# Taking TensorE's turns and bank waits one iteration later in a graph layer's edge loop

## The chip, the cores and the metric

The kernel runs on one core of a Trainium2 chip. The metric is the device time of one execution in microseconds, lower is better. The profile's names for the engines are used throughout: PE is TensorE, PEld its weight loads, DVE is VectorE, ACT is ScalarE, POOL is GpSimd, SP is SyncE. A *post* is the semaphore update by which an instruction tells the other engines that it is done.

## The reference

One layer of message passing over 12,500 nodes and 400,000 edges that are sorted by their destination, all in float32, residual added at the end:

```
h  = max(layernorm(x), 0)
y0 = h0 @ W_l1_0 * a ; y1 = h1 @ W_l1_1 * a          (nodes: 64 scalars, 32 vectors of 3)
w  = silu(edge16 @ fc_W1) @ fc_W2                    (edges: 192 weights each)
ys = y[edge_src]
mid = [w_a*ys0*e0, w_d*(ys1 . e1), (w_b*ys0) x e1, w_c*e0 x ys1]     (384 numbers an edge)
z  = zeros.at[edge_dst].add(mid)
out = x + C_S*(h @ W_sc * a) + C_X*(z @ W_l2 * a)
```

## The kernel before

A first stage goes over the nodes, writes the rows y to `y_d` in DRAM and keeps x plus the self term in `acc` in SBUF. Meanwhile POOL gathers rows of x for 22 batches whose y rows are made later on the chip instead of gathered (`gather_x`, L345).

Then comes the edge loop. The edges lie in 3,125 tiles of 128. Four tiles (`GT`) are a batch, so there are 782 batches, and iteration b of the loop issues work of several batches at once. The order on PE, ACT and DVE is written out by hand (`manual_schedule`): each engine runs its instructions in just the order in which the loop issues them. POOL runs ahead on its own.

- POOL: `load(b + 8)` issues four indirect DMAs, one a tile, that gather rows of y into a buffer `yg` (nine buffers). A buffer is free for the next gather when ACT has lifted it and DVE's `tmp` and `both` have read it. A made batch gathers nothing.
- PE: `weigh(b + 2)` makes the weights of a batch in one of two pairs of banks, `pw` (L566). It must wait until DVE has done the products of batch b, which read the same `pw`. `sums(b)` multiplies the products with a 0/1 selector and adds them in a bank `pz` (L603); a group of tiles shares one `pz` bank, 24 tiles (6 batches) in the first 1,824 tiles, called the wide part here, 12 tiles (3 batches) in the narrow part behind it. Two `pz` banks are used in turn.
- ACT: `pw` (L567) copies the edge's vector behind the weights as soon as `weigh` has posted; then it runs the evictions of `leaving`, that is what PE wrote in the iteration before (`all_leave`), then `yge` (L484), the lifting of the gathered rows. DVE can't begin a batch before ACT's `pw`.
- DVE: `dot` (L489, L491), `multiply` (L495 to L501), and every third batch `select` (L583), which makes the selector of 12 tiles by comparing the numbers 0 to 127 with the edges' relative destinations. The numbers lie in columns 384 to 511 of the `pz` banks.

At a group's end e, ACT evicts the sums in iteration e + 1 (`zs`, L609). PE turns them in the same iteration e + 1 (`turn`, L617), ACT evicts the turned sums at e + 2 (`za`, L621) and PE multiplies them with the output weights at e + 2 too (`map_sums`, L630). Turns, maps, the edge network's first layer (`hidden`, L550, in every second iteration) and the made batches' own turns and maps (L689, L700 to L702) all take the next of two shared banks `px`; so one iteration can use both, and a bank is used again as soon as ACT has evicted it.

The made batches are those with b a multiple of 32, up to 704.

Of the kernel before, what the change touches and what calls it, by code (L numbers as in the profile page):

```python
# [10 lines left out]
F32 = mybir.dt.float32  # L11
I32 = mybir.dt.int32
AF = mybir.ActivationFunctionType
ALU = mybir.AluOpType
# [4 lines left out]
P = 128  # L19
M0 = 64  # L20
M1 = 32
# [4 lines left out]
ZC = 384  # L26
GT = 4
BT = 32
WN = 128
TG = 12  # L30
EG = 8
WIDE = 3, 5
GN = 8
HN = 2
RB = 22
RS = 32
LO = D - P
EPS = 1e-5
C_S = math.sin(math.pi / 8.0)
# [4 lines left out]
def kernel(  # L44
# [19 lines left out]
    nc = tc.nc  # L64
# [36 lines left out]
    nr = max(0, min(RB, (NB - 1) // RS - 1))  # L101
    RT = nr * GT
    xr_d = dram.tile([max(nr, 1) * P, GT * D + 1], F32, name="xr_d")

    def made(b):

        return b // RS - 1 if b % RS == 0 and 0 < b <= nr * RS else None

    z_d = dram.tile([ZR, ZC], F32, name="z_d")

# [197 lines left out]
    with (  # L308
# [20 lines left out]

        def find_x():  # L330

            of = src_sb[:, RS * GT:RS * GT * (nr + 1)].rearrange("p (r c) -> p r c", c=RS * GT)[:, :, 0:GT]
            whole = nrp.tile([P, nr, GT], I32, name="whole")
            nc.vector.tensor_scalar(whole, of, 7, None, ALU.arith_shift_right)
            nc.vector.tensor_copy(hi_f.rearrange("p (r c) -> p r c", c=GT), whole)
            nc.vector.tensor_copy(lo_f.rearrange("p (r c) -> p r c", c=GT), of)
            nc.vector.scalar_tensor_tensor(lo_f, hi_f, -float(P), lo_f, op0=ALU.mult, op1=ALU.add)

        def gather_x(lo, hi):

            for r in range(lo, hi):
                xr = nrx.tile([P, GT * D + 1], F32, name="xr")
                for k in range(GT):
                    c = (r + 1) * RS * GT + k
                    nc.gpsimd.indirect_dma_start(  # L345
                        out=xr[:, k * D:(k + 1) * D], out_offset=None, in_=x,
                        in_offset=bass.IndirectOffsetOnAxis(ap=src_sb[:, c:c + 1], axis=0))
                xrs[r] = xr
# [134 lines left out]
        for k in range(n):  # L483
            nc.scalar.activation(yge[:, k, :], yg[:, k, :], AF.Copy, scale=e4v[:, k, 0:1])  # L484
# [8 lines left out]
    def multiply(pr, both, tmp, wt, yg, yge, n):  # L493

        nc.vector.tensor_mul(both[:, :n, :], wt[:, :n, 96:160], yg[:, :n, 0:M0])  # L495
# [5 lines left out]
        nc.vector.tensor_mul(pr[:, :n, 96:192].rearrange("p t (c u) -> p t c u", c=3),  # L501
                             wt[:, :n, M0:96].unsqueeze(2).to_broadcast([P, n, 3, M1]),
                             yge[:, :n, M0:].rearrange("p t (c u) -> p t c u", c=3))

    with (
# [15 lines left out]
        def next_px():  # L521
            turns["px"] += 1
            return pxs[turns["px"] % 2]
# [4 lines left out]
        def tiles_of(b):  # L528
            return list(range(b * GT, min((b + 1) * GT, T)))
# [46 lines left out]
            o = g % EG * TG + k * GT  # L576
            return raws[g // EG][:, o:o + GT, :]

        def select(u, pz):

            n = min(TG, T - u * TG)
            sels[u] = selp.tile([P, TG, WN], F32, name="sel")
            nc.vector.tensor_tensor(sels[u][:, 0:n, :], pz[:, ZC:].unsqueeze(1).to_broadcast([P, n, WN]),  # L583
                                    drel[:, u * TG:u * TG + n].unsqueeze(2).to_broadcast([P, n, WN]), ALU.is_equal)

        def dots_of(b):
            dots[b] = part.tile([P, GT, 4, M1], F32, name="tmp")
            dot(dots[b], wts[b], rows[b], len(tiles_of(b)))

        def products(b):  # L590
            pr = prod.tile([P, GT, ZC], F32, name="pr")
            both = part.tile([P, GT, M0], F32, name="both")
            multiply(pr, both, dots.pop(b), wts.pop(b), rows.pop(b), lifted.pop(b), len(tiles_of(b)))
            prs[b] = pr

        def sums(b):
# [15 lines left out]
        def turn(g):  # L612

            zs = z_sb.pop(g)
            pt = next_px()[:, 0:3 * P].rearrange("p (k c) -> p k c", k=3)
            for k in range(3):
                nc.tensor.transpose(pt[:, k, :], zs[:, P * k:P * (k + 1)], ident)  # L617

            def out_of():
                za = post.tile([P, 3, P], F32, name="za")  # L620
                nc.scalar.activation(za, pt, AF.Copy)  # L621
                zT[g] = za
            leaving.append(out_of)
# [97 lines left out]

        def plan(r):

            end = (r + 1) * RS - 9
            last = end - (end + 1) % 6
            first = last - 6 * (GT - 1)
            for when, b, f in ([(at_start, first - 6, made_load), (on_vector, first - 3, made_moments),
                                (on_vector, first - 1, made_reciprocal)]):
                when.setdefault(max(b, 0), []).append(lambda f=f: f(r))
            for k in range(GT):  # L730
                j = first + 6 * k
                for when, b, f in ((on_vector, j - 1, made_rows), (on_tensor, j, made_turn), (on_tensor, j + 2, made_map),
                                   (on_vector, j + 4, made_attr), (on_scalar, j + 5, made_leave)):
                    when.setdefault(b, []).append(lambda f=f, k=k: f(r, k))

        for r in range(nr):
# [13 lines left out]
        with order:  # L750
# [6 lines left out]
                all_leave()  # L757
            if NQ == 1:
                any_far(next_px()[0:1, 0:1])
            for b in range(min(2, NB)):  # L760
                weigh(b)
                lift_rows(b)
            for pz in pzs:
                nc.vector.tensor_copy(pz[:, ZC:], iota[:, 0:WN])
            dots_of(0)
            products(0)
            select(0, pzs[0])
# [47 lines left out]
    with (  # L815
# [11 lines left out]
        with tc.For_i(0, n, 1) as _:  # L827
# [4 lines left out]
            with tc.For_i(0, TP // GT, 1) as g:  # L832
# [31 lines left out]
                dot(tmp, pw, yg, GT)  # L864
                pr = fp.tile([P, GT, ZC], F32, name="f_pr")
                both = fp.tile([P, GT, M0], F32, name="f_both")
                multiply(pr, both, tmp, pw, yg, yge, GT)
# [81 lines left out]
```

## Time and profile before

| what | us |
|---|---|
| median of 3 runs | 5222.7 |
| lowest and highest run | 5202.25, 5230.44 |
| the profiled execution's own time | 5204.84 |
| its span, first to last instruction | 5203.0 |
| PE, DVE, POOL, ACT busy | 4180.4, 3441.9, 2959.6, 1764.7 |
| granted clock of TensorE, mean | 0.857 |

The span is that of one profiled execution. In rows of groups the columns are: line, engine, operation, out<-in by the program's names, shapes, xcount, then busy us and mean ns of one, then the engine's idle time just before them and what ended most of it. In rows of the timeline: start us, duration us, engine, line, operation, names, shapes, xcount, and in brackets the idle time before and what ended it. "issue" and "remote" mean that the profile shows nothing on this core's engines that ended the wait. The profile records a float32 matmul as two rows.

### The profile page before, as it was taken

Reading aid. Unit: us, or ns where it says so; the run is one execution under the profiler, and the core shown is the slowest. Engines: PE = TensorE matmul, PEld = TensorE weight load, DVE = VectorE, ACT = ScalarE, POOL = GpSimd, SP = SyncE. Lnnn points to the kernel's source line nnn. Section 1 sums busy time; section 2 is a strip of 40 time slices with the busy share of each in tenths; the row PEclk is TensorE's granted clock in tenths of the full one; section 3 lists DMA queues with packets and bytes.
Section 4 is the critical chain, followed back from the end, with each engine's and each line's share of the span. In section 5 each row is a group of like instructions: output and inputs, shape, how many; then the busy total and the mean of one; then the engine's idle time right before and its main releaser. Section 6 shows DMA issues by size and latency. Waiting matters only on the chain. (4 is left out here: it accounts for less than half of the span.)

```text
span 5203.0 us, 55078 instructions
## 1 busy us (share of the span) xinstructions
PE 4180.4 (80%) x16329; PEld 2384.2 (46%) x16329; DVE 3441.9 (66%) x7529; ACT 1764.7 (34%) x5580; POOL 2959.6 (57%) x3137
## 2 busy tenths in 40 slices
PE   4478888787888888888888878888888888888888
PEld 3334444444444444444444444444444444544444
DVE  4456667666666666776666666676767666766667
ACT  3323333333333333332333333333333333333333
POOL 4455655555555555555555555555555555655553
PEclk7778888888888888888888888888888888888888
DMA  5322222222222222222222222222222222232222
GB/s 180 115 57 58 61 58 62 58 60 60 57 60 59 60 61 57 59 61 60 57 60 58 60 57 57 60 60 58 60 54 61 58 59 57 61 94 57 57 57 58
DMA packets 227720, 333.84 MB, mean 64 GB/s; under 512 B 54714, under 2 KB 171526, under 8 KB 227158
## 3 DMA queue, kind: packets, MB, share of 16 engines
q0 software_dynamic: 150000, 256.20, 19.9%
q1 hardware_dynamic: 63618, 65.63, 4.0%
q10 hardware_dynamic: 13796, 8.44, 0.5%
q8 instruction: 130, 2.13, 0.2%
q14 instruction: 176, 1.44, 0.1%
HBM read 306.83 MB, written 23.22 MB: 63 GB/s over the span
## 5 line engine op out<-in xcount | busy, mean ns | idle before, releaser
L540 POOL DMA_INDIRECT yg<-y_d,src_sb x3037 | 2871.3, 945 | 2115.7 <-ACT yge L484 784.9
L603 PE MATMUL pz<-pr,sel 128*128 128x384 f32 x6250 | 2510.0, 548 | 58.4 <-issue 54.7
L603 PEld LDWEIGHTS pz<-pr,sel 128*128 128x128 f32 x6250 | 1259.2, 212 | 1032.0 <-issue 491.5
L489 DVE TENSOR_TENSOR tmp<-yg,pw 128x384 f32<-128x384 f32 x760 | 418.6, 551 | 1523.1 <-ACT pw L567 1292.7
L567 ACT ACTIVATE pw<-raw 128x12 f32<-128x12 f32 x782 | 141.9, 182 | 3289.3 <-issue 2801.2
L484 ACT ACTIVATE yge<-yg,raw 128x160 f32<-128x160 f32 x3037 | 1044.0, 421 | 0.0
L566 PE MATMUL pw<-w,hT 64*128 64x192 f32 x6250 | 839.5, 392 | 73.7 <-issue 24.1
L566 PEld LDWEIGHTS pw<-w,hT 64*128 64x128 f32 x6250 | 572.6, 212 | 545.1 <-issue 313.4
L497 DVE TENSOR_TENSOR pr<-both,pw 128x768 f32<-128x768 f32 x782 | 737.9, 944 | 0.0
L550 PE MATMUL px<-xe,w 32*128 32x512 f32 x782 | 522.9, 756 | 189.4 <-ACT os L635 137.1
L491 DVE TENSOR_REDUCE tmp<-tmp 128x128 f32<-128x384 f32 x782 | 464.1, 594 | 26.9
L583 DVE TENSOR_TENSOR sel<-pz,drel 128x1536 f32<-128x1536 f32 (+1 forms) x261 | 455.2, 1744 | 0.0
L501 DVE TENSOR_TENSOR pr<-pw,yge 128x384 f32<-128x384 f32 x782 | 428.0, 547 | 0.0
L617 PE MATMUL px<-ident,zs 128*128 128x128 f32 x555 | 112.7, 319 | 358.9 <-ACT zs L609 341.3
L500 DVE TENSOR_TENSOR pr<-pw,yge 128x256 f32<-128x256 f32 x782 | 326.6, 418 | 13.0 <-ACT yge L484 12.3
L495 DVE TENSOR_TENSOR both<-pw,yg 128x256 f32<-128x256 f32 x760 | 314.8, 414 | 0.0
L550 PEld LDWEIGHTS px<-xe,w 32*128 32x128 f32 x782 | 130.7, 209 | 345.5 <-ACT os L635 163.4
L630 PE MATMUL px<-wc,za 128*128 128x96 f32 x1110 | 165.5, 289 | 145.3 <-ACT za L621 137.7
L617 PEld LDWEIGHTS px<-ident,zs 128*128 128x128 f32 x555 | 74.2, 159 | 446.9 <-ACT zs L609 395.9
L630 PEld LDWEIGHTS px<-wc,za 128*128 128x128 f32 x1110 | 161.5, 205 | 207.4 <-ACT za L621 155.1
L555 ACT ACTIVATE hT<-px 128x512 f32<-128x512 f32 x391 | 229.3, 587 | 1.9 <-PE px L550 1.7
L496 DVE TENSOR_TENSOR pr<-pw,tmp 128x128 f32<-128x128 f32 x782 | 219.4, 281 | 0.0
(118 smaller groups left out, 1739.2 us busy)
## 6 DMA issues: line engine op xcount, KB each, us to landing
yg<-y_d,src_sb POOLq DMA_INDIRECT x3037
xe<-in_e SPq DMA_DIRECT2D x196, 128.0 KB
y_d<-ys ACTq DMA_DIRECT2D x12, 640.0 KB
xr_d<-xr SPq DMA_DIRECT2D x22, 320.5 KB
acc<-in_x SPq DMA_DIRECT2D x11, 640.0 KB
xm<-xr_d SPq DMA_DIRECT2D x22, 320.0 KB
out<-acc SPq DMA_DIRECT2D x11, 640.0 KB
raw<-in_e SPq DMA_DIRECT2D x32, 192.0 KB
```

The source lines that it names most:

```text
L484: nc.scalar.activation(yge[:, k, :], yg[:, k, :], AF.Copy, scale=e4v[:, k, 0:1])
L489: nc.vector.tensor_tensor(tmp[:, :n, 0:3, :], y1, wt[:, :n, NW:NW + 3].unsqueeze(3).to_broadcast([P, n, 3, M1]), ALU.mult)
L491: nc.vector.tensor_reduce(tmp[:, :n, 3, :], tmp[:, :n, 0:3, :].rearrange("p t c u -> p t u c"), AX.X, ALU.add)
L497: nc.vector.tensor_mul(pr[:, :n, 192:ZC].rearrange("p t (c u) -> p t c u", c=3), both[:, :n, :].unsqueeze(2).to_broadcast([P, n, 3, M0]), ...
L500: nc.vector.tensor_mul(pr[:, :n, 0:M0], wt[:, :n, 0:M0], yge[:, :n, 0:M0])
L501: nc.vector.tensor_mul(pr[:, :n, 96:192].rearrange("p t (c u) -> p t c u", c=3), wt[:, :n, M0:96].unsqueeze(2).to_broadcast([P, n, 3, M1]) ...
L540: nc.gpsimd.indirect_dma_start(out=yg[:, k, :], out_offset=None, in_=y_d, in_offset=bass.IndirectOffsetOnAxis(ap=src_sb[:, t:t + 1], axis=0))
L550: nc.tensor.matmul(ph, w1[r, :], xe[r, :], start=True, stop=True)
L566: nc.tensor.matmul(pw[:, k, 0:NW], hT[r, o:o + P], w2[r, :], start=True, stop=True)
L583: nc.vector.tensor_tensor(sels[u][:, 0:n, :], pz[:, ZC:].unsqueeze(1).to_broadcast([P, n, WN]), drel[:, u * TG:u * TG + n].unsqueeze(2).to ...
L603: nc.tensor.matmul(z_ps[g], sels[t // TG][:, t % TG, :], pr[:, k, :], start=first, stop=last)
L630: nc.tensor.matmul(px[:, lo:hi], za[:, k, :], wc[:, k, lo:hi], start=k == 0, stop=k == 1)
```

## The change

Sums' turns move. `turn(g)` comes at e + 2 in place of e + 1 and writes into the group's own `pz` bank, whose sums ACT has evicted an iteration before. `map_sums` follows at the next odd iteration at least two later, and the add to `acc` two after that; at the end of the program all three keep the old distance. The shared banks `px` are now used once an iteration: `hidden` in even iterations, maps and the made batches' turns and maps in odd ones. For this the made batches are spread anew: 16 of them 24 batches apart in the wide part (before 14, 32 apart), 6 of them 48 apart in the narrow part, where the four tiles of one are handled 12 iterations apart in place of 6, with 6 between turn and map in place of 2.

The numbers 0 to 127 for the selector leave `pz`: 32 of them lie behind the weights of each of the four tiles in both `pw` (column 224 on). `select` reads them there, in the bank of the batch that DVE is at, and comes between `dots_of` and `products` in place of behind `products`. `both` moves from `multiply` to `dot`, ahead of the reduction.

```diff
+SP = 256 - WN // 4
-RB = 22
-RS = 32
+RB = 16, 6
+RS = 24, 48
...
-    def dot(tmp, wt, yg, n):
+    def dot(tmp, both, wt, yg, n):
 
         y1 = yg[:, :n, M0:].rearrange("p t (c u) -> p t c u", c=3)
         nc.vector.tensor_tensor(tmp[:, :n, 0:3, :], y1, wt[:, :n, NW:NW + 3].unsqueeze(3).to_broadcast([P, n, 3, M1]),
                                 ALU.mult)
+        nc.vector.tensor_mul(both[:, :n, :], wt[:, :n, 96:160], yg[:, :n, 0:M0])
         nc.vector.tensor_reduce(tmp[:, :n, 3, :], tmp[:, :n, 0:3, :].rearrange("p t c u -> p t u c"), AX.X, ALU.add)
...
-            nc.vector.tensor_tensor(sels[u][:, 0:n, :], pz[:, ZC:].unsqueeze(1).to_broadcast([P, n, WN]),
-                                    drel[:, u * TG:u * TG + n].unsqueeze(2).to_broadcast([P, n, WN]), ALU.is_equal)
+            for_each = pw[:, :, SP:].unsqueeze(1).to_broadcast([P, n, GT, WN // GT])
+            nc.vector.tensor_tensor(sels[u][:, 0:n, :].rearrange("p t (k c) -> p t k c", k=GT), for_each,
+                                    drel[:, u * TG:u * TG + n].unsqueeze(2).unsqueeze(3).to_broadcast(
+                                        [P, n, GT, WN // GT]), ALU.is_equal)
...
-            pt = next_px()[:, 0:3 * P].rearrange("p (k c) -> p k c", k=3)
+            pt = pzs[g % 2][:, 0:3 * P].rearrange("p (k c) -> p k c", k=3)
...
-                turns_at.setdefault(e + 1, []).append(g)
-                maps_at.setdefault(e + 2, []).append(g)
-                adds_at.setdefault(e + (4 if e + 4 < NB else 3), []).append(g)
+                at_end = e + 4 >= NB
+                t = e + (1 if at_end else 2)
+                m = t + (1 if at_end else 2 if (t + 2) % 2 else 3)
+                turns_at.setdefault(t, []).append(g)
+                maps_at.setdefault(m, []).append(g)
+                adds_at.setdefault(m + (1 if at_end else 2), []).append(g)
...
                     dots_of(b + 1)
+                    if k == K - 1:
+                        select(u + 1, wts[b + 1])
                     products(b + 1)
-                    if k == K - 1:
-                        select(u + 1, pzs[(group_at[b * GT] + 1) % 2])
```

On PE, in the wide part, at a group's end. L603 is `sums`, L617 `turn`, L550 `hidden`, L566 `weigh`, L630 `map_sums`, L700 to L702 a made batch's map; the numbers tell the two `pz` and the two `px` apart. Before:

```order
L603 MATMUL pz_1674<-pr,sel 128x384 x4
L617 MATMUL px_1675<-ident,zs 128x128 x3
L550 MATMUL px_1676<-xe,w_98 128x512
L566 MATMUL pw_1672<-w_99,hT 128x192 x4
L603 MATMUL pz_1674<-pr,sel 128x384 x4
L630 MATMUL px_1675<-wc,za 128x96
L630 MATMUL px_1675<-wc,za 128x64
L630 MATMUL px_1675<-wc,za 128x96
L700 MATMUL px_1676<-wn_96,m_t 128x64
```

Changed, with the lines eight to twelve further down (L615 `sums`, L629 `turn`, L558 `hidden`, L574 `weigh`, L642 `map_sums`, L712 the made batch's map):

```order
L615 MATMUL pz_1675<-pr,sel 128x384 x4
L629 MATMUL pz_1676<-ident,zs 128x128 x3
L712 MATMUL px_1678<-wn_96,m_t 128x64
L713 MATMUL px_1678<-wn_97,m_t 128x96
L714 MATMUL px_1678<-a_sb,m_t 128x98
L574 MATMUL pw_1673<-w_99,hT 128x192 x4
L615 MATMUL pz_1675<-pr,sel 128x384 x4
L558 MATMUL px_1677<-xe,w_98 128x512
L574 MATMUL pw_1674<-w_99,hT 128x192 x4
L615 MATMUL pz_1675<-pr,sel 128x384 x4
L642 MATMUL px_1678<-wc,za 128x96
```

The turn now stands in the bank of the group that ended, while `sums` go to the other one; `hidden` has one `px` bank in even iterations, and the maps have the other in odd ones, with two iterations between turn and map.

On DVE, in a batch with a selector. L489 is the product for `tmp`, L491 its reduction, L495 `both`, L496 to L501 the products that PE sums, L583 `select`. Before:

```order
L489 TENSOR_TENSOR tmp<-yg,pw_1671 128x4x96
L491 TENSOR_REDUCE tmp<-tmp 128x4x32
L495 TENSOR_TENSOR both<-pw_1671,yg 128x256
L496 TENSOR_TENSOR pr<-pw_1671,tmp 128x4x32
L497 TENSOR_TENSOR pr<-both,pw_1671 128x4x192
L500 TENSOR_TENSOR pr<-pw_1671,yge 128x4x64
L501 TENSOR_TENSOR pr<-pw_1671,yge 128x4x96
L583 TENSOR_TENSOR sel<-pz_1673,drel 128x1536
```

Changed, with L497, L500 and L499 in place of L489, L491 and L495, L504 to L509 for the products and L592 for `select`:

```order
L497 TENSOR_TENSOR tmp<-yg,pw_1673 128x4x96
L499 TENSOR_TENSOR both<-pw_1673,yg 128x256
L500 TENSOR_REDUCE tmp<-tmp 128x4x32
L592 TENSOR_TENSOR sel<-pw_1673,drel 128x1536
L504 TENSOR_TENSOR pr<-pw_1673,tmp 128x4x32
L505 TENSOR_TENSOR pr<-both,pw_1673 128x4x192
L508 TENSOR_TENSOR pr<-pw_1673,yge 128x4x64
L509 TENSOR_TENSOR pr<-pw_1673,yge 128x4x96
```

The selector stands ahead of the four products, on whose last one PE's next `weigh` for that `pw` waits.

More of the change, by code (lines that the diff above doesn't have):

```diff
@@ L99 @@
     y_d = dram.tile([N, D], F32, name="y_d")
-    nr = max(0, min(RB, (NB - 1) // RS - 1))
+    n1 = max(0, min(RB[0], wide // GT // RS[0] - 2, (NB - 1) // RS[0] - 1))
+    from2 = wide // GT // RS[0] * RS[0] + RS[1]
+    n2 = max(0, min(RB[1], (NB - 1 - from2) // RS[1] + 1))
+    made_at = [RS[0] * (r + 2) for r in range(n1)] + [from2 + RS[1] * r for r in range(n2)]
+    nr = n1 + n2
     RT = nr * GT
@@ L105, in made @@
     def made(b):
-        return b // RS - 1 if b % RS == 0 and 0 < b <= nr * RS else None
+        return made_at.index(b) if b in made_at else None
     z_d = dram.tile([ZR, ZC], F32, name="z_d")
@@ L330, in find_x @@
         def find_x():
-            of = src_sb[:, RS * GT:RS * GT * (nr + 1)].rearrange("p (r c) -> p r c", c=RS * GT)[:, :, 0:GT]
             whole = nrp.tile([P, nr, GT], I32, name="whole")
-            nc.vector.tensor_scalar(whole, of, 7, None, ALU.arith_shift_right)
+            for r, n, step in ((0, n1, RS[0]), (n1, n2, RS[1])):
+                if n:
+                    c = made_at[r] * GT
+                    of = src_sb[:, c:c + ((n - 1) * step + 1) * GT].rearrange("p (m c) -> p m c", c=GT)[:, ::step, :]
+                    nc.vector.tensor_scalar(whole[:, r:r + n, :], of, 7, None, ALU.arith_shift_right)
+                    nc.vector.tensor_copy(lo_f[:, r * GT:(r + n) * GT].rearrange("p (r c) -> p r c", c=GT), of)
             nc.vector.tensor_copy(hi_f.rearrange("p (r c) -> p r c", c=GT), whole)
-            nc.vector.tensor_copy(lo_f.rearrange("p (r c) -> p r c", c=GT), of)
             nc.vector.scalar_tensor_tensor(lo_f, hi_f, -float(P), lo_f, op0=ALU.mult, op1=ALU.add)
@@ L343, in gather_x @@
                 for k in range(GT):
-                    c = (r + 1) * RS * GT + k
+                    c = made_at[r] * GT + k
                     nc.gpsimd.indirect_dma_start(
@@ L490, in dot, with multiply @@
                                 ALU.mult)
+        nc.vector.tensor_mul(both[:, :n, :], wt[:, :n, 96:160], yg[:, :n, 0:M0])
         nc.vector.tensor_reduce(tmp[:, :n, 3, :], tmp[:, :n, 0:3, :].rearrange("p t c u -> p t u c"), AX.X, ALU.add)
-    def multiply(pr, both, tmp, wt, yg, yge, n):
-        nc.vector.tensor_mul(both[:, :n, :], wt[:, :n, 96:160], yg[:, :n, 0:M0])
+    def multiply(pr, both, tmp, wt, yge, n):
         nc.vector.tensor_mul(pr[:, :n, M0:96], wt[:, :n, 160:NW], tmp[:, :n, 3, :])
@@ L722, in plan @@
         def plan(r):
-            end = (r + 1) * RS - 9
+            b = made_at[r]
+            step, lag = (6, 2) if b * GT <= wide else (12, 6)
+            end = b - 7 - lag
             last = end - (end + 1) % 6
-            first = last - 6 * (GT - 1)
+            first = last - step * (GT - 1)
             for when, b, f in ([(at_start, first - 6, made_load), (on_vector, first - 3, made_moments),
@@ L730, in plan @@
             for k in range(GT):
-                j = first + 6 * k
-                for when, b, f in ((on_vector, j - 1, made_rows), (on_tensor, j, made_turn), (on_tensor, j + 2, made_map),
-                                   (on_vector, j + 4, made_attr), (on_scalar, j + 5, made_leave)):
+                j = first + step * k
+                for when, b, f in ((on_vector, j - 1, made_rows), (on_tensor, j, made_turn), (on_tensor, j + lag, made_map),
+                                   (on_vector, j + lag + 2, made_attr), (on_scalar, j + lag + 3, made_leave)):
                     when.setdefault(b, []).append(lambda f=f, k=k: f(r, k))
@@ L759 @@
                 any_far(next_px()[0:1, 0:1])
+            for pw in pws:
+                nc.vector.tensor_copy(pw[:, :, SP:], iota[:, 0:WN].rearrange("p (k c) -> p k c", k=GT))
             for b in range(min(2, NB)):
@@ L762 @@
                 lift_rows(b)
-            for pz in pzs:
-                nc.vector.tensor_copy(pz[:, ZC:], iota[:, 0:WN])
             dots_of(0)
+            select(0, wts[0])
             products(0)
-            select(0, pzs[0])
             last_batch = [(t - 1) // GT for t in ends]
@@ L863 @@
                 tmp = fp.tile([P, GT, 4, M1], F32, name="f_tmp")
-                dot(tmp, pw, yg, GT)
                 pr = fp.tile([P, GT, ZC], F32, name="f_pr")
                 both = fp.tile([P, GT, M0], F32, name="f_both")
-                multiply(pr, both, tmp, pw, yg, yge, GT)
+                dot(tmp, both, pw, yg, GT)
+                multiply(pr, both, tmp, pw, yge, GT)
                 for k in range(GT):
```

12 lines of the change are left out of this document (7 added, 5 removed).

## The prediction

> **What bounds the kernel now.** I read the page first: its first line, then the groups of POOL's gathers and of ACT's `pw`.
>
> ```profile
> PE 4180.4 (80%) x16329; PEld 2384.2 (46%) x16329; DVE 3441.9 (66%) x7529; ACT 1764.7 (34%) x5580; POOL 2959.6 (57%) x3137
> L540 POOL DMA_INDIRECT yg<-y_d,src_sb x3037 | 2871.3, 945 | 2115.7 <-ACT yge L484 784.9 <-issue 782.1 <-ACT pw L567 161.0
> L567 ACT ACTIVATE pw<-raw 128x12 f32<-128x12 f32 x782 | 141.9, 182 | 3289.3 <-issue 2801.2
> ```
>
> PE is the busiest engine and still idle for a fifth of the span. ACT is idle far longer, 3289.3 us of it in front of `pw`, most of it put down to nothing. The list of PE's waits says for what, with total us, times and longest:
>
> ```profile
> PE px L617 <- ACT zs L609: 341.3, 82, 9.7
> PE px L630 <- ACT za L621: 137.7, 27, 9.8
> PE px L550 <- ACT os L635: 137.1, 37, 6.1
> PE px L689 <- ACT os L635: 65.3, 17, 6.6
> ```
>
> These are just the waits that the change is made for: 341.3 + 137.7 + 137.1 + 65.3 = 681 us in 163 waits. The question is whether they are a cause or a symptom. They are 4.2 us in the mean, with single ones near 10. So I looked at ACT, which does the evictions behind `pw`, in the timeline from 2040 to 2080 us, and at POOL and PE beside it, one fence each:
>
> ```profile
> 2050.26 0.18 ACT L567 ACTIVATE pw<-raw 128x12 f32<-128x12 f32 x1 [7.47 <-issue]
> 2050.37 0.47 ACT L609 ACTIVATE zs<-pz 128x384 f32<-128x384 f32 x1
> ...
> 2078.46 0.18 ACT L567 ACTIVATE pw<-raw 128x12 f32<-128x12 f32 x1 [9.75 <-issue]
> ```
>
> ```profile
> 2049.84 0.94 POOL L540 DMA_INDIRECT yg<-y_d,src_sb  x1 [0.30 <-issue]
> 2052.72 0.94 POOL L540 DMA_INDIRECT yg<-y_d,src_sb  x1 [1.94 <-issue]
> ...
> 2075.16 0.95 POOL L540 DMA_INDIRECT yg<-y_d,src_sb  x1 [0.30 <-issue]
> ```
>
> ```profile
> 2043.43 0.92 PE L566 MATMUL pw<-w,hT 64*128 64x192 f32 x8
> 2044.28 2.85 PE L603 MATMUL pz<-pr,sel 128*128 128x384 f32 x8
> 2050.90 0.90 PE L617 MATMUL px<-ident,zs 128*128 128x128 f32 x3 [3.77 <-ACT zs L609]
> 2051.73 2.07 PE L550 MATMUL px<-xe,w 32*128 32x512 f32 x2
> 2053.73 1.65 PE L566 MATMUL pw<-w,hT 64*128 64x192 f32 x8
> 2055.32 5.16 PE L603 MATMUL pz<-pr,sel 128*128 128x384 f32 x8
> ...
> 2069.35 0.92 PE L566 MATMUL pw<-w,hT 64*128 64x192 f32 x8
> ...
> 2072.98 1.12 PE L550 MATMUL px<-xe,w 32*128 32x512 f32 x2
> 2074.03 0.92 PE L566 MATMUL pw<-w,hT 64*128 64x192 f32 x8
> ```
>
> ACT's `pw` at 2050.26 needs the `weigh` that PE shows as ended at 2043.43 + 0.92 = 2044.35. It starts 5.9 us later, when POOL has come to the end of a run of gathers. PE's wait for `zs`, an eviction of 0.47 us, is the tail of that wait. At 2078.46 it is the same, 8.2 us behind the `weigh` of 2069.35, and there PE waited for no eviction: it went on to `hidden` and the next `weigh`, and ACT still stood until POOL's run had ended at 2075.16 + 0.95. So a `weigh`'s post reaches ACT late while POOL issues gathers, whether PE waits or not.
>
> The first stage shows this by itself. ACT's L405 there waits for PE's turns:
>
> ```profile
> 24.26 0.60 ACT L405 ACTIVATE hT<-pt 128x512 f32<-128x512 f32 x1 [2.10 <-issue]
> 51.61 0.60 ACT L405 ACTIVATE hT<-pt 128x512 f32<-128x512 f32 x1 [25.60 <-remote]
> ```
>
> ```profile
> 25.30 0.27 PE L399 MATMUL pt<-ident,h 128*128 128x128 f32 x1
> ```
>
> ```profile
> 24.74 0.95 POOL L345 DMA_INDIRECT xr<-in_x,src_sb  x1 [0.30 <-issue]
> ...
> 51.01 0.95 POOL L345 DMA_INDIRECT xr<-in_x,src_sb  x1 [0.30 <-issue]
> ```
>
> PE's turns ended at 25.57 and ACT got to them at 51.61, with POOL gathering all the while. The Trainium skill, Perfetto Trace Analysis, section Per-instruction lifecycle, says that a matmul's end in a profile is an estimate and that the propagation of its semaphore is hidden from it; the traces agree in that nothing here shows why the post is late.
>
> Last, does the own-iteration wait set the pace? The wide part has half as many turns a batch as the narrow part. The stretches before and after 3132 us, for `sums` alone, and then the turns of each (PE's groups by stretch):
>
> ```profile
> 232.00:3132.00 2900.00, 1467.91 (x3632) 733.58 (x3632) 0.85 0.23 59
> 3132.00:5180.00 2048.00, 1032.48 (x2592) 520.93 (x2592) 0.87 0.24 61
> L617 PE MATMUL px<-ident,zs 128*128 128x128 f32 x225 | 48.8, 336 | 222.7 <-ACT zs L609 205.8 <-ACT pw L567 14.2 <-issue 2.7
> L617 PE MATMUL px<-ident,zs 128*128 128x128 f32 x321 | 62.4, 309 | 136.2 <-ACT zs L609 135.5 <-issue 0.7
> ```
>
> Eight rows of `sums` are a batch: 454 batches at 6.39 us, then 324 at 6.32. The turns are 75 in the first stretch (0.17 a batch) and 107 in the second (0.33). Twice the turns, and no slower. What both stretches share is POOL: four gathers at 0.945 + 0.30 are 4.98 us a batch, and POOL's pause at the end of each run, while ACT gets its post and frees buffers, makes the rest.
>
> **The change part by part.** I work against the profiled execution, 5204.84 us; the median of the runs, 5222.7, is 17.9 above it.
>
> *Turns, maps and `hidden` an iteration later.* PE's instructions stay the same in number. The 681 us of waits go or shrink; the question is what they held up. In a stall PE would now do the turn and `hidden` that it did behind it, and `weigh`'s next post comes earlier by up to 0.90 + 2.07 = 2.97 us (the rows at 2050.90 and 2051.73, cold). 163 times that is 484 us if all of it reaches the pace. The two stretches say none of it does. The pair in the timeline says all: from the release at 2050.26, where PE had waited, to that at 2078.46 four batches took 28.2 us. I take a fifth, since whole stretches weigh more than one place: **-97**, with bounds 0 and -484. ACT's own wait for `weigh`, on which DVE, then `yge`, then POOL's buffers wait, is untouched.
>
> By the Trainium skill, TensorE: Matmul & The Clock Gate, section HAM oscillation, gaps over some 3.4 us put the array back to half its clock; the row of 5.16 us for `sums` behind the gap of 3.77 us, against 2.85, agrees.
>
> *The turn in the sums' bank* adds a wait: the first `sums` of the next group but one must wait until ACT has emptied the turned sums. In the narrow part that eviction is in the iteration just before, in the wide part four iterations earlier. Queued behind it on PE is one `sums` group. Bounds: 0, and 107 groups by 2.85 = 305 us if each met a stall; I take 0, since the `weigh` ahead of it waits for the same stalled ACT through DVE. The Trainium skill's Perfetto Trace Analysis, section Matmuls, would have independent groups rotate through banks, which speaks against this; by it the sum would be nearer the upper bound.
>
> *`select` ahead of the products.* DVE's work is the same 1536 elements, at 1744 ns:
>
> ```profile
> L583 DVE TENSOR_TENSOR sel<-pz,drel 128x1536 f32<-128x1536 f32 (+1 forms) x261 | 455.2, 1744 | 0.0
> PEld pw L566 <- DVE pr L501: 41.1, 49, 1.5
> PE pz L603 <- DVE sel L583: 3.2, 6, 0.7
> ```
>
> In 260 batches the last product, for which `weigh` waits, comes 1.744 us later, and with it the post that ACT waits for. At most that is 453 us. It is hidden where PE is still at `sums` (2.85 us). The second row, from the waits of PE's weight loads, names the products 49 times in 782 `weigh`s, one in sixteen; 260/16 by 1.744 is 28. I take **+30**, bounds 0 and 453. In return `sums` need not wait for the selector (third row): **-3**. Reading the numbers from `pw` in four pieces may be slower or faster; no row has it, and by the elements it is the same.
>
> *`both` ahead of the reduction* gives a gather buffer free one reduction sooner on DVE, but POOL's row of the page names ACT's engine for its waits, `yge` for 784.9 us, and DVE not at all: 0. *Made batches* stay 22 with 88 turns; their loads go to SP's queue some iterations earlier, with nothing waiting there: 0.
>
> Sum: -97 + 30 - 3 = -70. 5204.84 - 70 = 5135, and with the 17.9 of the runs **5153 us**.
>
> **The rivals.**
>
> *The waits are the cause.* Then half to all of the 681 us goes: 5222.7 - 681 = 4542 to 4882. For it: PE is the busiest, and warm PE work is far below the span. Against it: the two stretches, and the stall at 2069 to 2078, in which PE waited for nothing.
>
> *The idle only moves.* PE gets to the next `weigh` and waits there for DVE, which waits for ACT, which waits for the post; what PE did early is lost again. Then the time is that of before, 5223, within 26 us. For it: again the stretches.
>
> *`select` holds the posts back.* A stalled kernel catches up by DVE: behind a release two batches are ready, and DVE works without a pause while PE waits for its products. There the 1.744 us are bare, and a post that comes later falls deeper into POOL's run, where it waits longer. Break-even is (97 + 3)/1.744 = 57 of the 260 selectors; with 100 bare the sum is -100 + 174 = +74, 5297 us, with half of them +127, 5350. For it: the two stalls above last until POOL pauses, so a lost post costs microseconds. Against it: the one in sixteen.
>
> **How the numbers follow.** My forecast has 0.37, the waits as the cause 0.15, the idle that moves 0.14, `select` holding the posts 0.34. About 0.5%, 26 us, is what a measurement of this kernel can tell from no change. The forecast and the first rival are faster by more, nearly all of them; the second is the same; the third is slower. This gives faster 0.51, same 0.14, slower 0.35. The range begins at 4900, where two thirds of the 484 us reach the pace (-323) or half of the 681, and ends at 5350, half of the selectors bare. Outside are most of the first rival and the tail of the third, together 0.2. The forecast's own range is 5000 to 5200.
>
> **What would show it.** Right: PE's waits for `zs`, `za` and `os` nearly gone, but ACT's idle time before `pw` still near the 3289.3 us of before, POOL still in runs with pauses, and PE's idle now in front of `weigh`, put down to DVE. If `select` bites, DVE's products are named ahead of `weigh` far more often than 49 times. Wrong: ACT's idle before `pw` down by hundreds of us, which would mean that PE's waits made the posts late.

## The result, and the profile after

| | before | after |
|---|---|---|
| median of 6 runs, us | 5216.09 | 5169.81 |
| lowest and highest, us | 5202.25, 5230.44 | 5156.79, 5179.38 |
| profiled execution, us | 5204.84 | 5158.47 |
| mean granted clock | 0.857 | 0.862 |

The ratio is 0.9909, with a 95% interval of 0.9885 to 0.9934: 0.9% less, where the prediction had 1.3% less. A later group of runs gave 0.9937 [0.9913, 0.9961].

The page of after, its first line and the groups of POOL's gathers and of ACT's `pw` (L575 now, L567 before):

```profile
PE 4206.4 (82%) x16329; PEld 2396.3 (46%) x16329; DVE 3407.8 (66%) x7531; ACT 1751.1 (34%) x5580; POOL 2968.1 (58%) x3137
L548 POOL DMA_INDIRECT yg<-y_d,src_sb x3037 | 2880.6, 949 | 2049.0 <-ACT pw L575 1017.9
L575 ACT ACTIVATE pw<-raw 128x12 f32<-128x12 f32 x782 | 140.8, 180 | 3256.7 <-issue 2215.6
```

ACT's idle time ahead of `pw` is 3256.7 us where it was 3289.3. The posts of `weigh` come late as often as they did: counted over each trace, `pw` starts more than 1.5 us behind the later of its `weigh`'s end and ACT's instruction before it in 266 of 781 batches before, and in 266 after. The waits of PE have other names, though (the last row is from the waits of PE's weight loads):

```profile
PE pz L615 <- ACT za L633: 259.6, 82, 5.7
PE pw L574 <- issue: 221.9, 237, 12.5
PE pw L574 <- DVE pr L509: 135.3, 92, 4.9
PE pz L629 <- ACT zs L621: 7.5, 5, 3.0
PE px L642 <- ACT za L633: 4.7, 4, 1.7
PEld pw L574 <- DVE pr L509: 180.2, 114, 4.3
```

`turn` (L629) waits 7.5 us for `zs` where it waited 341.3, and `map_sums` (L642) 4.7 us for `za` where it waited 137.7. The waits of `hidden` and of the made batches' turns for `os` (137.1 and 65.3 us) are down to 0.2 us in all. In their place, `sums` (L615) now wait 259.6 us for `za`, since the turned sums lie in their bank, and `weigh` (L574) waits for DVE's products or for nothing that is shown. The stretches that hold the same counts of `sums` as the two of before, 3,632 and 2,592 rows, tell where the time came from:

```profile
226.00:3072.00 2846.00, 1509.39 (x3632) 740.62 (x3632) 0.87 0.24 60
3072.00:5134.00 2062.00, 1123.09 (x2592) 557.33 (x2592) 0.86 0.24 60
```

The wide part takes 2846 us where it took 2900, so 54 less. The narrow part takes 2062 us where it took 2048, so 14 more. The narrow part has fewer made batches than before, though, 6 in place of 8, and so more to gather. POOL's gathers in that stretch, before and after:

```profile
L540 POOL DMA_INDIRECT yg<-y_d,src_sb x1238 | 1170.7, 946 | 852.7 <-ACT yge L484 375.8 <-issue 305.2 <-ACT pw L567 89.7
L548 POOL DMA_INDIRECT yg<-y_d,src_sb x1247 | 1182.2, 948 | 850.8 <-ACT pw L575 478.1 <-issue 328.0 <-DVE pr L509 19.5
```

By the gather the stretch takes 2048 / 1238 = 1.65 us before and 2062 / 1247 = 1.65 us after. Two more gathered batches are eight gathers, 8 x 1.65 = 13 us by this estimate, and in the wide part they are saved. So the 14 us are no more than they bring at the old pace, and do not show what the new wait costs. The timeline of after shows such a wait in the narrow part, PE, then ACT, then POOL's last gather of its run:

```profile
3171.26 0.92 PE L574 MATMUL pw<-w,hT 64*128 64x192 f32 x8
...
3174.89 1.12 PE L558 MATMUL px<-xe,w 32*128 32x512 f32 x2
3175.94 0.92 PE L574 MATMUL pw<-w,hT 64*128 64x192 f32 x8
3180.61 5.13 PE L615 MATMUL pz<-pr,sel 128*128 128x384 f32 x8 [3.75 <-ACT za L633]
```

```profile
3179.97 0.18 ACT L575 ACTIVATE pw<-raw 128x12 f32<-128x12 f32 x1 [10.32 <-issue]
3180.09 0.47 ACT L633 ACTIVATE za<-pz 128x384 f32<-128x384 f32 x1
```

```profile
3176.71 0.94 POOL L548 DMA_INDIRECT yg<-y_d,src_sb  x1 [0.30 <-issue]
```

ACT takes the `weigh`s in their order, and the `pw` at 3179.97 is that of the `weigh` at 3171.26. This one ended at 3171.26 + 0.92 = 3172.18, so `pw` comes 7.8 us later, 2.3 us behind the end of POOL's run. Meanwhile PE has run `hidden` and the next `weigh`. `za`, written behind `pw` on ACT, comes with it, and PE stands until then. The eviction itself takes 0.47 us.

### The profile page after: what moved, and what is told of

Read it like the earlier page. It is cut to its first block, busy times and chain, and to the rows that moved or that the text cites. A ratio compares the mean times of both kernels' runs of the same rounds, so it can differ in the third digit from the quotient of the medians.

```text
span 5156.7 us, 54940 instructions
## 1 busy us (share of the span) xinstructions
PE 4206.4 (82%) x16329; PEld 2396.3 (46%) x16329; DVE 3407.8 (66%) x7531; ACT 1751.1 (34%) x5580; POOL 2968.1 (58%) x3137
## 5 line engine op out<-in xcount | busy, mean ns | idle before, releaser
L615 PE MATMUL pz<-pr,sel 128*128 128x384 f32 x6250 | 2641.6, 569 | 377.8 <-ACT za L633 259.6
L615 PEld LDWEIGHTS pz<-pr,sel 128*128 128x128 f32 x6250 | 1302.6, 219 | 1424.4 <-issue 663.1
L497 DVE TENSOR_TENSOR tmp<-yg,pw 128x384 f32<-128x384 f32 x760 | 416.8, 548 | 1533.7 <-ACT pw L575 1405.0
L575 ACT ACTIVATE pw<-raw 128x12 f32<-128x12 f32 x782 | 140.8, 180 | 3256.7 <-issue 2215.6
L574 PE MATMUL pw<-w,hT 64*128 64x192 f32 x6250 | 855.4, 368 | 380.9 <-issue 221.9
L574 PEld LDWEIGHTS pw<-w,hT 64*128 64x128 f32 x6250 | 558.0, 196 | 773.1 <-issue 494.1
L558 PE MATMUL px<-xe,w 32*128 32x512 f32 x782 | 444.6, 650 | 26.1 <-ACT hT L563 13.4
L592 DVE TENSOR_TENSOR sel<-pw,drel 128x1536 f32<-128x1536 f32 (+1 forms) x261 | 454.7, 1742 | 0.0
L500 DVE TENSOR_REDUCE tmp<-tmp 128x128 f32<-128x384 f32 x782 | 454.6, 581 | 0.0
L509 DVE TENSOR_TENSOR pr<-pw,yge 128x384 f32<-128x384 f32 x782 | 426.2, 545 | 0.0
L499 DVE TENSOR_TENSOR both<-pw,yg 128x256 f32<-128x256 f32 x760 | 316.0, 416 | 0.0
L504 DVE TENSOR_TENSOR pr<-pw,tmp 128x128 f32<-128x128 f32 x782 | 224.3, 287 | 18.0
L558 PEld LDWEIGHTS px<-xe,w 32*128 32x128 f32 x782 | 117.0, 187 | 231.9 <-issue 179.6
L642 PEld LDWEIGHTS px<-wc,za 128*128 128x128 f32 x1110 | 153.8, 198 | 78.3 <-ACT m_p L718 28.4
L642 PE MATMUL px<-wc,za 128*128 128x96 f32 x1110 | 154.4, 276 | 27.8 <-ACT m_p L718 19.7
L660 DVE SCALAR_TENSOR_TENSOR acc<-os,by,acc 128x160 f32 x370 | 142.3, 385 | 14.4 <-ACT os L647 1.1
L406 PE MATMUL pt<-ident,h 128*128 128x128 f32 x98 | 30.6, 332 | 111.1 <-issue 58.8
```

Source lines behind the costliest of these rows:

```text
L558: nc.tensor.matmul(ph, w1[r, :], xe[r, :], start=True, stop=True)
L574: nc.tensor.matmul(pw[:, k, 0:NW], hT[r, o:o + P], w2[r, :], start=True, stop=True)
L592: nc.vector.tensor_tensor(sels[u][:, 0:n, :].rearrange("p t (k c) -> p t k c", k=GT), for_each, drel[:, u * TG:u * TG + n].unsqueeze(2).un ...
L615: nc.tensor.matmul(z_ps[g], sels[t // TG][:, t % TG, :], pr[:, k, :], start=first, stop=last)
```

## The experiments

Each group of runs had the kernel before beside it on its own chip, and ratios are to that. The chips differ: before took 3963.51 us in the one run on the first group's chip, and 5212.38 and 5271.6 us (medians) on the next two.

**Is it the gathers that make the posts late?** First before, and then after, with every batch reading one buffer that is filled once:

```diff
+    still = ygp.tile([P, GT, D], F32, name="still")
+    nc.vector.memset(still, 0.5)
...
-            yg = ygp.tile([P, GT, D], F32, name="yg")
-            rows[b] = yg
-            for k, t in enumerate(tiles_of(b)):
-                nc.gpsimd.indirect_dma_start(
...
+            rows[b] = still
```

> The kernel before, with no row gathered in the edge loop: every batch reads one buffer filled once with 0.5, so the messages are not the reference's; all other work stands. Theory 1 (POOL's gathers hold PE's posts back, and ACT, DVE and PE wait for that): ACT's idle time before pw falls from 3289 us to under 1800, no wait of PE for zs, za or os is over 3 us, and the time falls to what PE's own work takes, 4100 to 4500 us. Theory 2 (PE's waits for evictions of its own iteration set the pace by themselves): the waits stay near 681 us, the time stays above 4900.

> The changed kernel with the same part left out (no row gathered in the loop). Theory 1: within 150 us of the kernel before without gathers, either way, since with prompt posts an own-iteration eviction costs PE about 1 us in 163 to 300 places. Theory 2: below the kernel before without gathers by 400 us or more, because the own-iteration waits are gone in it.

Then after with plain loads of neighbouring rows, issued by SP and, in one more kernel, by POOL (`nc.gpsimd` in place of `nc.sync`):

```diff
-                nc.gpsimd.indirect_dma_start(
-                    out=yg[:, k, :], out_offset=None, in_=y_d,
-                    in_offset=bass.IndirectOffsetOnAxis(ap=src_sb[:, t:t + 1], axis=0))
+                r0 = t * P % (N - P)
+                nc.sync.dma_start(yg[:, k, :], y_d[r0:r0 + P, :])
```

> The changed kernel with each gather replaced by a plain load of 128 neighbouring rows of y, issued from SP: the same bytes into the same buffers, but wrong rows, and POOL idle in the loop. If it is POOL's part in a gather that holds the posts back (theory 1a), the time comes near that without gathers, under 4500 us. If it is the traffic of the rows as such (theory 1b), posts stay late, ACT's idle before pw stays above 2800 us and the time above 4900.

> As the one before it, but the plain loads of neighbouring rows are issued from POOL. Theory 1a in its wide form (any DMA issued by POOL holds PE's posts): ACT's idle before pw stays above 2500 us, the time above 4800. In its narrow form (only the gather by a list of rows does): under 4500 us. The time of one issue on POOL is open; if it is well under 0.95 us, something in between.

Measured, one run each: 3680.38 us for before without gathers, 3677.93 for after without them, 3681.44 with SP's loads, 3694.79 with POOL's. The first lines of the two pages without gathers, before's and after's:

```profile
PE 3611.5 (98%) x16329; PEld 2128.0 (58%) x16329; DVE 3415.6 (93%) x7530; ACT 1772.8 (48%) x5580; POOL 97.4 (3%) x100
```

```profile
PE 3607.2 (98%) x16329; PEld 2127.7 (58%) x16329; DVE 3399.5 (92%) x7532; ACT 1773.8 (48%) x5580; POOL 97.3 (3%) x100
```

Without gathers PE is busy for 98% of both spans, and the change is worth 2.45 us, 0.07%, which single runs cannot tell from nothing. ACT's idle time before `pw` is 1830.1 us in the first of them, just above the 1800 that was expected, and the time is far below the expected 4100 to 4500. But before itself took only 3963.51 us on that chip, so these runs alone do not say where the 1500 us of the slower chips go.

Their first stage says more. In it POOL gathers rows of x in all these kernels. POOL's group and ACT's one wait for PE's turns, on the first chip:

```profile
L347 POOL DMA_INDIRECT xr<-in_x,src_sb x88 | 94.6, 1075 | 27.9 <-issue 24.6 <-DMA src_sb<-in_src 1.5 <-DVE st L368 0.9
ACT hT L407 <- ACT ys L426: 0.4, 1, 0.4
```

In the profile of before this stage has a wait of ACT of 25.60 us. Here a gather's issue takes 1075 ns in the mean, no less than the 972 there, the gathers stand as close, 0.30 us apart, in runs as long, and no post is late. So on this chip a run of gathers did not hold back PE's posts, and kernels that ran on it cannot show what does on the others. The kernel with POOL's plain loads was therefore run again, last of all, in a group where before took 5267.2 us:

> Once more after with plain loads of 128 neighbouring rows, issued by POOL in place of its gathers by a list (the rows are not those of the list; transfers, buffers and waits for the rows stay), because the first group ran on a chip where the kernel before took only 3963.51 us. Theory 1 (the gathers by a list on POOL hold back PE's posts): where before takes 5200 us, this kernel still takes about 3690 us (3650 to 3800), PE busy 98 per cent at a clock near 0.99, its waits for evictions gone: what differs between the chips is then what a gather costs. Theory 2 (the waits are of the order's making, and the chip of the first group was faster in all): the time stays above 4700 us with the sums' wait for za at 200 us or more.

Measured: 3752.63 us, ratio 0.7123 [0.7103, 0.7144]. Its page's first line, POOL's group, and two rows of the waits of PE:

```profile
PE 3612.4 (96%) x16329; PEld 2132.9 (57%) x16329; DVE 3408.4 (91%) x7531; ACT 1774.1 (47%) x5580; POOL 1699.5 (45%) x3137
L549 POOL DMA_DIRECT2D yg<-y_d x3037 | 1609.6, 537 | 1948.6 <-ACT yge L492 1366.3 <-issue 283.8 <-ACT pw L574 186.2
PE pw L573 <- DVE pr L509: 4.5, 2, 4.0
PE px L641 <- ACT za L632: 0.6, 1, 0.6
```

The order on PE, ACT and DVE is that of after, POOL still issues 3,037 transfers of the same size into the same buffers, and the evictions wait for the same posts. Yet PE's waits for evictions and products in the loop are under 10 us in all, the time is 1515 us below that of before, and `pw` is late by the count above in none of 781 batches. In the same execution the first stage still gathers by a list, and there ACT still waits for PE's turns:

```profile
ACT hT L413 <- remote: 63.3, 6, 28.4
```

So theory 1 holds on this chip: the gathers by a list on POOL make the waits. What differs between the chips is not the time of a gather's issue: in the first stage it is 979 ns here, against the 1075 on the first chip.

Where in a run a post falls matters. Counting as one run what stands less than 0.7 us apart, POOL's runs last 13.9 us in the mean in after's trace. There 249 of the 386 `weigh`s that end 6 to 15 us into a run are late, 12 of the 248 that end earlier in one, and 1 of the 117 outside of runs; 170 of the late `pw` start 2 to 3 us behind the run's end. POOL's runs also end because no buffer is free, and buffers wait for ACT, so a trace alone would not tell which holds which; the plain loads do. What they leave open is whether it is the form of the transfer or the length of the run, because a plain issue takes 537 ns in place of 949, and POOL's runs last 2.1 us in the mean and 5.0 at most with them.

**Before and after once more, with their parts.** Before and after unchanged:

> The kernel before once more, for its profile beside the others of this group. Theory 1 (POOL's indirect gathers hold back the posts of PE's products): where the kernel before takes some 5216 us, PE waits some 680 us for evictions of its own iteration; on a chip where it takes about 3960 us, only some 280 us above the 3680 us that the kernels without gathers took there, those waits are far below 300 us although the order is the same. Theory 2 (the own-iteration waits are made by the order of PE and ACT): they stay between 500 and 700 us on any chip.

> The kernel after once more, beside its parts. Theory 1: 0.991 of before where before takes 5216 us; where before takes some 3960 us there is less lateness to take from, and the ratio is between 0.995 and 1.01. Theory 2: 0.99 or less on either chip.

Measured: 5215.45 us, 1.0017 [0.9998, 1.0035], and 5174.49 us, 0.9937 [0.9913, 0.9961]. This chip was one of the slower ones, so the waits of the two kernels with gathers on the first chip were not seen. The waits of PE in the repeat of before, and of after:

```profile
PE px L617 <- ACT zs L609: 345.4, 85, 9.7
PE px L630 <- ACT za L621: 170.5, 28, 9.8
```

```profile
PE pz L615 <- ACT za L633: 292.1, 89, 5.9
```

They are the same waits within some tens of us.

After with the turn in a shared bank, at the iteration where after has it:

```diff
-            pt = pzs[g % 2][:, 0:3 * P].rearrange("p (k c) -> p k c", k=3)
+            pt = next_px()[:, 0:3 * P].rearrange("p (k c) -> p k c", k=3)
```

> After, with the turns at the iteration where after has them but back in a shared bank, so that the first sums of the next but one group do not wait for za. If that wait (259.6 us in the profile after) is real time: the narrow part gets back its 14 us and more, 0.2 to 1 per cent below after in the same group. If the wait only shows idle that a late post would make anyway (theory 1 in its strict form): equal to after within 0.2 per cent, with PE's idle moved to another row.

Measured: 5214.72 us, 1.0006 [0.9988, 1.0024]. All that after gains is gone, against both expectations, although turns, maps and adds are as late as in after. The waits of PE show it:

```profile
PE px L558 <- ACT za L633: 356.0, 76, 7.5
PE px L712 <- ACT za L633: 52.5, 23, 4.1
PE px L701 <- ACT za L633: 30.1, 9, 4.2
```

The same late `za` now holds `hidden` and the made batches' steps, for 438.6 us in place of the 292.1 us of the `sums`. So against a shared bank the turn's bank is not a cost of after's, as the upper bound of the prediction had it, but a part that pays: 5214.72 - 5174.49 = 40 us. What is left of the change adds up to nothing that these runs can tell: later turns, the selector and the new made batches together.

Before with only the later iterations for turn, map and add:

```diff
-                turns_at.setdefault(e + 1, []).append(g)
-                maps_at.setdefault(e + 2, []).append(g)
-                adds_at.setdefault(e + (4 if e + 4 < NB else 3), []).append(g)
+                at_end = e + 4 >= NB
+                t = e + (1 if at_end else 2)
+                m = t + (1 if at_end else 2 if (t + 2) % 2 else 3)
+                turns_at.setdefault(t, []).append(g)
+                maps_at.setdefault(m, []).append(g)
+                adds_at.setdefault(m + (1 if at_end else 2), []).append(g)
```

> Before with one part alone: turns, maps and additions at the later iterations that after has, in the shared banks as before; selector, both and the made batches as before. Theory 1 and theory 2 both want the gain here: the ratio to before is as after's or lower (0.985 to 0.992 where before takes 5216 us). The rival that after gains by its selector or its made batches: 0.998 or more.

Measured: 5170.9 us, 0.9934 [0.9911, 0.9958]. It does not answer its question. With the made batches of before, a turn, a map and a made batch's step can fall into one iteration of the narrow part, and then the third overwrites a shared bank ahead of its eviction, so that waits are missing which a complete kernel has.

**ACT's order, the selector, the made batches.** In after, `weigh` and its `pw` moved behind `all_leave` and what `on_scalar` is due, so that ACT evicts first:

```diff
-                if b + 2 < NB:
-                    weigh(b + 2)
                 all_leave()
                 due(on_scalar, b)
+                if b + 2 < NB:
+                    weigh(b + 2)
```

> After, with ACT's evictions of the iteration behind written ahead of the weigh and its numbers, so that za, zs and the shared banks do not leave behind a copy that waits for a weigh's late post. If the sums' wait for za (292.1 us in the repeat of after) is an order of ACT's own making: it falls below 60 us and the kernel takes 0.5 to 2 per cent less than after in its group. If a late post of PE's is what holds it (theory 1), ACT waits in the same place for the post of the turn or the hidden step instead, and DVE's products start later: within 0.3 per cent of after where posts come late, PE's idle moved to the weigh's wait for DVE. Rival on the other side: the weights' numbers now stand behind evictions that wait for PE's last step, and the kernel is 0.5 to 2 per cent slower than after.

Measured: 5115.17 us, 0.9705 [0.969, 0.972], faster than both kernels. Rows of the waits of PE, ACT's groups of `pw`, `za` and `zs`, and the two stretches:

```profile
PE pw L574 <- ACT yge L492: 116.0, 40, 4.2
PE pw L574 <- DVE pr L509: 91.3, 46, 13.4
PE pz L615 <- ACT za L633: 8.5, 3, 3.8
```

```profile
L575 ACT ACTIVATE pw<-raw 128x12 f32<-128x12 f32 x782 | 143.9, 184 | 1028.8 <-remote 446.5 <-PE pw L574 198.3 <-issue 149.1
L633 ACT ACTIVATE za<-pz 128x384 f32<-128x384 f32 x185 | 89.9, 486 | 585.1 <-remote 203.3 <-issue 140.6 <-PE pz L629 74.5
L621 ACT ACTIVATE zs<-pz 128x384 f32<-128x384 f32 x185 | 89.2, 482 | 487.6 <-remote 296.7 <-PE pz L615 65.4 <-issue 63.6
```

```profile
229.00:3085.00 2856.00, 1525.04 (x3632) 750.68 (x3632) 0.87 0.24 60
3085.00:5103.00 2018.00, 1083.53 (x2592) 536.68 (x2592) 0.88 0.25 62
```

After itself did not run on this chip. The next kernel did, which is after but for the place of the selector; its two stretches, one batch later:

```profile
232.00:3114.00 2882.00, 1519.83 (x3640) 748.24 (x3640) 0.87 0.24 60
3114.00:5199.00 2085.00, 1129.01 (x2584) 560.43 (x2584) 0.85 0.24 59
```

The sums' wait for `za` is 8.5 us. ACT now takes its late posts in front of `za` and `zs` too (585.1 and 487.6 us), while PE, whose order is unchanged, can go on. Only 1028.8 us are left in front of `pw`, on which DVE and the buffers depend, and `pw` is late by the count above in 154 batches in place of 266. ACT's idle time in all is hardly less, though, 5125.7 - 1814.9 = 3311 us by its page, against 5156.7 - 1751.1 = 3406 in after. Most of the gain is in the narrow part: 67 us, although with one batch more in it, against 26 in the wide part with one batch less. The strict form of theory 1 falls here: ACT stands about as long whatever the order, but what it has written behind a late post is a matter of order, and it is worth some 2%.

The selector behind the products:

```diff
-                    if k == K - 1:
-                        select(u + 1, wts[b + 1])
+                    pw = wts[b + 1]
                     products(b + 1)
+                    if k == K - 1:
+                        select(u + 1, pw)
```

> After, with the selector written behind the products that it stands ahead of there, still read from the numbers behind the weights. The prediction's term (the selector ahead delays a weigh in 1 of 16 cases, 30 us) wants this kernel 0.6 per cent faster than after, with PE's weigh and its load put down to DVE's products far fewer than the 92 and 114 times of after. The other way round: the weights' bank is now held by the selector for 1.74 us more in every third batch, so that the weigh waits for DVE's selector: equal or up to 0.5 per cent slower.

Measured: 5213.48 us, 0.9891 [0.9875, 0.9907]. After did not run on this chip; its own intervals, 0.9885 to 0.9934 and 0.9913 to 0.9961, overlap this one or lie just above it. A gain of 0.6% is not shown, and one of 0.2 to 0.5% not excluded. The waits of PE's `weigh`:

```profile
PE pw L574 <- DVE pr L509: 110.7, 69, 14.3
PE pw L574 <- DVE sel L592: 46.9, 23, 5.9
```

Together 157.6 us in 92 waits, where after had 135.3 us in 92. Part of the wait only takes the selector's name.

The made batches of before in after:

```diff
-    made_at = [RS[0] * (r + 2) for r in range(n1)] + [from2 + RS[1] * r for r in range(n2)]
+    n1, n2 = max(0, min(22, (NB - 1) // 32 - 1)), 0
+    made_at = [32 * (r + 1) for r in range(n1)]
...
-            step, lag = (6, 2) if b * GT <= wide else (12, 6)
+            step, lag = 6, 2
```

> After, with the made batches of before: one at every 32nd batch throughout, steps of 6 batches, map two batches behind the turn. The prediction's term for them is 0: equal to after within 0.2 per cent. The rival, from the run with the late turns in before (0.9934 of before, against 1.0006 for the turns in shared banks within after): the made batches of after cost what that difference is, and this kernel takes 0.3 to 0.7 per cent less than after.

Measured: 5184.05 us, 0.9838 [0.9823, 0.9852], 29 us below the selector's kernel on the same chip and below both intervals of after. The waits of PE:

```profile
PE pw L575 <- DVE pr L510: 199.6, 108, 16.7
PE pz L616 <- ACT za L634: 109.5, 33, 5.7
PE px L559 <- ACT os L648: 72.3, 14, 7.5
```

These rows are of an execution of 5206.39 us, the longest of the five. The sums wait for `za` 109.5 us, in 33 places in place of 82. So the new spread of the made batches costs some 0.5 to 1% within after, as far as ratios of different chips can be set side by side. This holds although with the old spread a map of the sums and one of a made batch can again fall into one iteration of the narrow part, and `hidden` waits 72.3 us for `os`. The posts are not less often late: `pw` is, by the count above, in 291 batches. Why the sums meet fewer of them with the old spread was not tried.

## Why the prediction was right, and where it was not

*The waits are mostly a symptom*: right. Over 90% of the waits for `zs` and of the maps for `za` went, and only 46 us of time with them. ACT's idle time before `pw` stayed, and with plain loads in after the waits went while its order on PE, ACT and DVE stayed. The rival that the waits are the cause (4542 to 4882 us) is out: even the best order found takes 2.95% off.

*Turns, maps and `hidden` an iteration later, -97*: right in sign; its size was not measured alone. The turn's bank brought 40 us of it. Without that bank the change comes to 1.0006, and if the made batches cost the 29 us below and the selector nothing, the later turns bring about as much, some 70 us for both. The fifth of 484 us that gave -97 was a choice between the bounds, which no row fixed, so that it came near is luck. The working was off, too: it priced the PE work that moves into a stall, while the runs show that what counts is which step meets the late eviction next, and what stands behind a late post on ACT.

*The turn in the sums' bank, 0 of 0 to 305*: mis-sized as a wait. It measured 259.6 us in 82 waits; what these cost in time was not measured alone, since the 14 us of the narrow part go with its two more gathered batches. The reason given for 0, that the `weigh` ahead waits for the same stalled ACT, failed in the timeline above: at 3175.94 the `weigh` ahead of the `sums` ran without a wait, while ACT still stood before the `pw` of the `weigh` before it, and the `sums` met the stall alone. The Trainium skill, Perfetto Trace Analysis, section Matmuls, advises rotating independent groups through banks so that evictions overlap; the row of 259.6 us agrees, for a turn in one of only two sums' banks. But the shared banks cost more.

*`select` ahead, +30*: not shown. DVE's products are named 114 times by the weight loads where it was 49, the sign that the prediction gave for this rival, but putting the selector back did not lessen the waits, 157.6 us against 135.3. The rival of 5297 us and more is out.

*Made batches, 0*: the step that failed. The prediction looked at their count and their loads, and not at where their gathers are spared. They cost about 29 us by the selector's kernel on the same chip, which differs in the selector too, and up to 52 by the ratios, (0.9937 - 0.9838) x 5216. Why stays open.

*The sum*: -70 against -46 measured. By the figures above turns with their bank brought some 70 us where 97 was put, the selector shows no cost where 30 was put, and the made batches cost about 29 where 0 was put. Each of the three is off by some 30 us, and two of them cancel: that the sum is off by no more than one of its terms is luck.

The clock: the rows of `sums` behind the waits are cold in after too, 5.13 us against 2.85. In the page with plain loads PE's busy time is 3612.4 us against after's 4206.4 for the same instructions, and the clock 0.983 against 0.862; so some 594 us of after's busy PE is what the lower clock adds, an estimate from these two pages. The Trainium skill, TensorE: Matmul & The Clock Gate, section HAM oscillation, says that idle gaps of more than some 3.4 us put PE back to half its clock; the rows behind the gaps agree, 5.13 us behind one of 3.75.

## What to carry to other kernels

When many waits end together, look for the one post that they all stand behind before giving each a price; moving the consumers mostly renames them, here for 0.9%. What can be moved with profit is the queue behind the late post: here the evictions in front of the copy that waits, for two swapped lines and 2%. And a bank that is shared by several steps made each of them wait for the latest eviction here, 438.6 us of waits against 292.1 with a bank apart.

## What the runs showed of the hardware

- On the slower chips PE's posts to ACT come late, in a third of the batches by over 1.5 us (266 of 781), while POOL issues gathers by a list, 949 ns each with 0.30 us between, in runs of 13.9 us in the mean. Of the 266 late ones in after's trace, 249 belong to a `weigh` that ended 6 to 15 us into a run, and 170 reach ACT 2 to 3 us behind the run's end. With plain transfers of the same size from POOL, 537 ns each in runs of 2.1 us, none of 781 was late. On one chip before takes 5267.2 us, and after with the plain transfers 3752.63.
- This differs between chips. Before took 3963.51 us on one of them, in one run, and 5212 to 5272 on the others. On the first, gathers of the first stage with the same 0.30 us between them held back none of 49 posts, where 6 of 49 were late by over 1.5 us in before's profile. After with POOL's plain loads took 3694.79 on the first and 3752.63 on another. Why was not found.
